# Four output stores per batch tile instead of five, through the same circular buffer

## The chip, the cores and the metric

One core of one Trainium2 chip. The metric is the device time of one execution in microseconds (us), median of several runs, lower is better. Each set of runs has the kernel before in its own rounds (medians 1341.10 to 1341.41 us), and every kernel is compared with that one unless the text says otherwise.

## The reference, cut to what matters

A pairwise bilinear interaction over 32 fields of 64 numbers, for a batch of 4096. Every pair (i, j) with i < j has its own 64 x 64 matrix.

```python
i_idx, j_idx = np.triu_indices(32, k=1)          # 496 pairs
vi, vj = inputs[:, i_idx, :], inputs[:, j_idx, :]
vdotw = jnp.einsum('bpd,pde->bpe', vi, W)
return (vdotw * vj).reshape(B, -1)               # 4096 x 31744 f32, 520 MB
```

The output is 520 MB and the input 42 MB. The work is in writing the result.

## The kernel before

The batch is cut into 32 tiles of 128 rows, one row for each SBUF partition. Fields are taken two at a time ("pair p" is fields 2p and 2p + 1, p = 0 to 15). TensorE multiplies into PSUM (the memory that takes its results), VectorE multiplies that by x and writes the product into a circular buffer (the ring), and the sync engine sends each finished stretch of the ring to HBM. One store carries the pairs of one group, so its row in each partition is the sum of their widths.

```python
STORES = [[0, 1], [2, 3], [4, 5], [6, 7, 8], [9, 10, 11, 12, 13, 14, 15]]
PREFETCH_AT = [5, 6]       # pairs at which the next tile is transposed
RING = 28160               # f32 words in each partition, 110 KB
...
for t in range(NT):
    ...                                            # x of tile t + 1 is loaded (ScalarE's queue)
    for s, group in enumerate(STORES):
        if at + store_w[s] > RING:
            at = 0                                 # the rest of the ring is skipped
        osb = ring[:, at : at + store_w[s]]
        at += store_w[s]
        for p in group:
            ...                                    # matmuls -> PSUM; VectorE: osb = PSUM * x
        nc.sync.dma_start(out=out[ts(t, P), o0 : o0 + store_w[s]], in_=osb)
```

A VectorE instruction that writes a stretch of the ring must wait until the older stores that read that stretch have landed. All pairs of a tile together are 31744 words, more than the ring holds.

Of the kernel before, what the change touches and what calls it, by code (L numbers as in the profile page):

```python
# [1 line left out]

# [6 lines left out]

F32 = mybir.dt.float32  # L10
ALU = mybir.AluOpType

P = 128
BANK = 512

STORES = [[0, 1], [2, 3], [4, 5], [6, 7, 8], [9, 10, 11, 12, 13, 14, 15]]
PREFETCH_AT = [5, 6]
RING = 28160


@with_exitstack
def pair_bilinear_kernel(
    ctx: ExitStack,
    tc: tile.TileContext,
    x: bass.AP,
    w: bass.AP,
    out: bass.AP,
    F: int,
    D: int,
):  # L30
















    nc = tc.nc
    B = x.shape[0]
    NT = B // P
    NPR = F // 2  # L50

    width = [(F - 1 - i) * D for i in range(F)]
    off = [sum(width[:i]) for i in range(F)]
    woff = [sum(width[0 : 2 * p : 2]) for p in range(NPR)]
    store_w = [sum(width[2 * p] + width[2 * p + 1] for p in g) for g in STORES]

    const = ctx.enter_context(tc.tile_pool(name="const", bufs=1))
    xpool = ctx.enter_context(tc.tile_pool(name="x", bufs=2))
    xtpool = ctx.enter_context(tc.tile_pool(name="xT", bufs=2))
    psum = ctx.enter_context(tc.tile_pool(name="ps", bufs=4, space=bass.MemoryType.PSUM))  # L60

    ident = const.tile([P, P], F32, tag="ident", name="ident")
    make_identity(nc, ident)

    def runs(tl, a, b, n):

        ap = tl[:, a : a + n]
        return bass.AP(ap.tensor, ap.offset, [list(ap.ap[0]), [b - a, 2], list(ap.ap[1])])

    def load_x(t):  # L70
        xt = xpool.tile([P, F * D], F32, tag="x", name=f"x_{t}")
        nc.scalar.dma_start(out=xt, in_=x[ts(t, P), :])
        return xt

    def transpose_x(xT, t, xt, g):

        n = 2 * BANK // P
        pt = psum.tile([P, 2 * BANK], F32, tag="ps", name=f"pt_{t}_{g}")
        for c in range(n):
            nc.tensor.transpose(pt[:, ts(c, P)], xt[:, ts(n * g + c, P)], ident)  # L80
        nc.scalar.copy(xT[:, ts(g, 2 * BANK)], pt)  # L81

    def new_xT(t):
        return xtpool.tile([P, NPR * P], F32, tag="xT", name=f"xT_{t}")

    ring = const.tile([P, RING], F32, tag="ring", name="ring")
    at = 0
    xs = {0: load_x(0)}

    w_sb = []  # L90
    for p in range(NPR):
        wp = const.tile([P, width[2 * p]], F32, tag=f"w{p}", name=f"w{p}")
        nc.sync.dma_start(out=wp, in_=w[:, woff[p] : woff[p] + width[2 * p]])
        w_sb.append(wp)

    xTs = {0: new_xT(0)}
    for g in range(2):
        transpose_x(xTs[0], 0, xs[0], g)

    for t in range(NT):  # L100
        xt, xT = xs.pop(t), xTs.pop(t)
        if t + 1 < NT:
            xs[t + 1] = load_x(t + 1)
        for s, group in enumerate(STORES):
            if at + store_w[s] > RING:
                at = 0
            osb = ring[:, at : at + store_w[s]]
            at += store_w[s]
            o0 = off[2 * group[0]]
            for p in group:  # L110
                if t + 1 < NT and p in PREFETCH_AT:
                    if t + 1 not in xTs:
                        xTs[t + 1] = new_xT(t + 1)
                    transpose_x(xTs[t + 1], t + 1, xs[t + 1], PREFETCH_AT.index(p))
                for c0 in range(0, width[2 * p], BANK):
                    pm = psum.tile([P, 2, BANK], F32, tag="ps", name=f"pm_{t}_{p}_{c0}")
                    n = [max(0, min(BANK, width[2 * p + h] - c0)) for h in range(2)]
                    for h in range(2):
                        if n[h]:
                            nc.tensor.matmul(  # L120
                                pm[:, h, : n[h]],
                                xT[h * D : (h + 1) * D, ts(p, P)],
                                w_sb[p][h * D : (h + 1) * D, c0 : c0 + n[h]],
                                start=True,
                                stop=True,
                            )
                    o = [off[2 * p + h] - o0 + c0 for h in range(2)]
                    xj = [(2 * p + h + 1) * D + c0 for h in range(2)]
                    if n[0] == n[1]:
                        nc.vector.tensor_tensor(  # L130
                            runs(osb, o[0], o[1], n[0]),
                            pm[:, :, : n[0]],
                            runs(xt, xj[0], xj[1], n[0]),
                            ALU.mult,
                        )
                    else:
                        for h in range(2):
                            if n[h]:
                                nc.vector.tensor_tensor(  # L139
                                    osb[:, o[h] : o[h] + n[h]],  # L140
                                    pm[:, h, : n[h]],
                                    xt[:, xj[h] : xj[h] + n[h]],
                                    ALU.mult,
                                )
            nc.sync.dma_start(out=out[ts(t, P), o0 : o0 + store_w[s]], in_=osb)


# [33 lines left out]
```

## Time and profile before

| | before |
|---|---|
| time, median of 3 | 1341.25 us (1340.96 to 1341.39) |
| DMA, mean over the span | 420 GB/s |
| VectorE, TensorE busy | 88%, 86% |
| VectorE's wait for ring space | 93.0 us in 53 waits |
| store, issue to landing (median) | 22.4 us |

How to read it: each row of a store is one packet in the DMA records, 128 rows over 16 DMA engines are 8 rows an engine, and a store has landed when all 16 engines are done. The lines are shown in the prediction.

### The profile page before, as it was taken

Reading aid. Unit: us, or ns where it says so; the run is one execution under the profiler, and the core shown is the slowest. Engines: PE = TensorE matmul, PEld = TensorE weight load, DVE = VectorE, ACT = ScalarE, POOL = GpSimd, SP = SyncE. Lnnn points to the kernel's source line nnn. Section 1 sums busy time; section 2 is a strip of 40 time slices with the busy share of each in tenths; the row PEclk is TensorE's granted clock in tenths of the full one; section 3 lists DMA queues with packets and bytes.
Section 4 is the critical chain, followed back from the end, with each engine's and each line's share of the span. In section 5 each row is a group of like instructions: output and inputs, shape, how many; then the busy total and the mean of one; then the engine's idle time right before and its main releaser. Section 6 shows DMA issues by size and latency. Waiting matters only on the chain.

```text
span 1339.7 us, 13755 instructions
## 1 busy us (share of the span) xinstructions
PE 1151.0 (86%) x5376; PEld 548.7 (41%) x5376; DVE 1177.4 (88%) x1664; ACT 66.1 (5%) x65; POOL 0.7 (0%) x6
## 2 busy tenths in 40 slices
PE   7998889888898888988888978889798897888992
PEld 3444344443343443443433534444344443444441
DVE  6999889888899988989888989899898997898993
ACT  1000000000000000000000000000000000000000
POOL 0000000000000000000000000000000000000000
PEclk9999889999999999989999899899898998998996
DMA  9999999999999999999999999999999999999996
GB/s 392 426 431 434 429 431 429 427 427 434 426 434 430 422 422 430 422 424 429 415 426 424 426 426 404 415 420 431 428 420 408 431 427 431 416 424 420 422 429 264
DMA packets 30017, 562.93 MB, mean 420 GB/s; under 512 B 3456, under 2 KB 3840, under 8 KB 5376
## 3 DMA queue, kind: packets, MB, share of 16 engines
q1 hardware_dynamic: 25344, 528.49, 92.6%
q10 hardware_dynamic: 4608, 33.56, 6.0%
q8 instruction: 42, 0.69, 0.2%
q14 instruction: 23, 0.19, 0.0%
HBM read 41.94 MB, written 520.09 MB: 420 GB/s over the span
## 4 chain that ended last, share of the span: by engine, by line
DMA 54%; DVE 23%; PE 11%; issue 9%; DVEq 0%
DMA out_dram<-ring 54%; DVE ring L130 15%; PE pm L120 9%; DVE ring L139 9%; PE pt L80 2%; DMA x<-in_x_dram 1%; DVEq L130 0%; DVEq L177 0%
## 5 line engine op out<-in xcount | busy, mean ns | idle before, releaser
L120 PE MATMUL pm<-w,xT 64*128 64x512 f32 (+7 forms) x4864 | 1083.2, 559 | 158.3 <-DVE ring L130 140.1
L130 DVE TENSOR_TENSOR ring<-pm,x 128x1024 f32<-128x1024 f32 x768 | 904.0, 1217 | 138.4 <-DMA out_dram<-ring 93.0
L120 PEld LDWEIGHTS pm<-w,xT 64*128 64x128 f32 x4864 | 487.7, 194 | 720.1 <-DVE ring L130 451.3
L139 DVE TENSOR_TENSOR ring<-pm,x 128x448 f32<-128x448 f32 (+6 forms) x896 | 330.2, 415 | 3.6 <-PE pm L120 2.9
L81 ACT COPY xT<-pt 128x1024 f32<-128x1024 f32 x64 | 64.8, 1012 | 1194.6 <-PE pt L80 1194.6
L80 PE MATMUL pt<-ident,x 128*128 128x128 f32 x512 | 76.5, 297 | 8.5 <-DMA x<-in_x_dram 8.5
L80 PEld LDWEIGHTS pt<-ident,x 128*128 128x128 f32 x512 | 61.0, 152 | 48.9 <-issue 35.3
L81 ACT ACT_TABLE_LOAD x1 | 1.3, 1283 | 1.7 <-PEq L173 1.7
masks.py:199 POOL TENSOR_SCALAR_AFFINE_SELECT ident<-ident 128x128 f32<-128x128 f32 x1 | 0.3, 292 | 0.1
masks.py:197 POOL MEMSET ident<- 128x128 f32 x1 | 0.2, 204 | 0.3 <-POOLq L173 0.3
L173 POOL MEMSET const-bfloat16-1.0<- 128x1 bf16 x1 | 0.1, 101 | 0.0
L173 POOL MEMSET const-uint8-127<- 128x1 uint8 x1 | 0.1, 101 | 0.0
L173 POOL MEMSET const-float32-0.0<- 128x1 f32 x1 | 0.1, 98 | 0.2 <-issue 0.2
L173 POOL MEMSET const-float32-1.0<- 128x1 f32 x1 | 0.1, 98 | 0.0
## 6 DMA issues: line engine op xcount, KB each, us to landing
out_dram<-ring SPq DMA_DIRECT2D x32, 3776.0 KB, 22.8
out_dram<-ring SPq DMA_DIRECT2D x32, 3264.0 KB, 21.8
out_dram<-ring SPq DMA_DIRECT2D x32, 3168.0 KB, 22.4
out_dram<-ring SPq DMA_DIRECT2D x32, 2912.0 KB, 22.3
out_dram<-ring SPq DMA_DIRECT2D x32, 2752.0 KB, 22.1
x<-in_x_dram ACTq DMA_DIRECT2D x32, 1024.0 KB, 14.2
w<-in_w_dram SPq DMA_DIRECT2D x1, 992.0 KB, 7.4
w<-in_w_dram SPq DMA_DIRECT2D x1, 928.0 KB, 11.7
```

What stands on the lines that cost most here:

```text
L80: nc.tensor.transpose(pt[:, ts(c, P)], xt[:, ts(n * g + c, P)], ident)
L81: nc.scalar.copy(xT[:, ts(g, 2 * BANK)], pt)
L120: nc.tensor.matmul(pm[:, h, : n[h]], xT[h * D : (h + 1) * D, ts(p, P)], w_sb[p][h * D : (h + 1) * D, c0 : c0 + n[h]], start=True, stop=True,)
L130: nc.vector.tensor_tensor(runs(osb, o[0], o[1], n[0]), pm[:, :, : n[0]], runs(xt, xj[0], xj[1], n[0]), ALU.mult,)
L139: nc.vector.tensor_tensor(osb[:, o[h] : o[h] + n[h]], pm[:, h, : n[h]], xt[:, xj[h] : xj[h] + n[h]], ALU.mult,)
L173: nc = bacc.Bacc("TRN2", target_bir_lowering=False, num_devices=1)
```

## The change

Its intent: one transfer fewer in each tile, and longer rows (26 to 39 KB instead of 22 to 30 KB), so less overhead on the queue that sets the time. Pair 6 moves to the third store, and the last two stores become one.

```diff
-STORES = [[0, 1], [2, 3], [4, 5], [6, 7, 8], [9, 10, 11, 12, 13, 14, 15]]
+STORES = [[0, 1], [2, 3], [4, 5, 6], [7, 8, 9, 10, 11, 12, 13, 14, 15]]
```

## The prediction

> **What bounds the kernel now.** I read the page's engine sums first, then the slices, the DMA queues, the chain, and last the waits and the closing 40 us.
>
> ```profile
> PE 1151.0 (86%) x5376; PEld 548.7 (41%) x5376; DVE 1177.4 (88%) x1664; ACT 66.1 (5%) x65; POOL 0.7 (0%) x6
> ...
> PEclk9999889999999999989999899899898998998996
> DMA  9999999999999999999999999999999999999996
> ...
> q1 hardware_dynamic: 25344, 528.49, 92.6%
> q10 hardware_dynamic: 4608, 33.56, 6.0%
> q8 instruction: 42, 0.69, 0.2%
> ...
> DMA out_dram<-ring 54%; DVE ring L130 15%; PE pm L120 9%; DVE ring L139 9%; PE pt L80 2%; DMA x<-in_x_dram 1%; DVEq L130 0%; DVEq L177 0%
> ```
>
> The DMA row is at 9 or above in every slice but the last, and the queue shares add to about 99%. VectorE and TensorE are at 88% and 86%: behind, but not far. The chain goes through stores for 54% and through VectorE and TensorE for the rest, so I need to know whether those stretches are a second limit or only a filled-up ring seen from the other side.
>
> ```profile
> PEld pm L120 <- DVE ring L130: 451.3, 535, 4.2
> ...
> DVE ring L130 <- DMA out_dram<-ring: 93.0, 53, 3.3
> DVE ring L130 <- PE pm L120: 45.4, 52, 13.2
> ```
>
> VectorE waits 93 us for ring space, that is for a store to land, and 45 us for TensorE, of which 13 are the start. Tile 0 has no ring waits and takes VectorE 36.9 us; a tile in the middle takes about 41. So compute is faster than the stores, and the ring throttles it.
>
> ```profile
> DMA  9999989998972999999999989893000000100000
> GB/s 422 392 422 412 422 351 585 404 404 356 422 334 92 406 406 406 406 402 529 576 426 395 395 371 400 375 584 165 25 25 25 23 23 23 47 23 23 23 0 0
> ...
> out_dram<-ring SPq DMA_DIRECT2D x1, 2752.0 KB, 22.4
> ```
>
> This is the window of the last 40 us, one slice a microsecond. After 1328 us the DMA moves about 25 GB/s: one engine of 16 is alone for ten more microseconds. From the trace's packet records, the last rows of each store on that engine end about 1.5 us after the others in tile 0, 8 us after at 550 us, and stay near 10 from then on. One engine falls behind, and a store has landed only when that one is done; the others then run dry waiting for the ring. So the bound is **the one late DMA engine**, and it never runs dry: each of its rows follows the last one directly to 1338.4.
>
> Its account: the packets of the big stores are whole rows, with median durations 818, 865, 940, 968 and 1119 ns for 22016, 23296, 25344, 26112 and 30208 B. A line through the shortest and longest has 301 ns for 8192 B (27.2 B/ns) and leaves 818 - 22016 x 0.03674 = 9 ns per row. Each engine carries 8 rows of each store: 8 x 4710 = 37.68 us a tile, plus 8 rows of x at 309 ns (2.47) and six 9 ns completion packets: 40.2. Times 32: 1286.6. The weights are 20.6 (8 x the sum of 16 medians). That is 1307 for any engine. The 42 instruction fetches of 16 KB are 42 x 16384 / 27.2 = 25.3 us if all sit on one engine, which would make the late one. Sum 1332.5; the first packet comes at 2 us, the last ends at 1338.4, so some 4 us are start-up gaps. The account closes.
>
> **What the Trainium skill says.** "DMA: Bandwidth & Descriptors", section "Specifications", gives 435 GB/s for 16 engines; 16 x 27.2 B/ns is 435, so the trace agrees and the engines already run at their ceiling inside a row. The same page, section "Why a DMA increments its semaphore by 16 and not by 1": only the full 16 means that all data landed; the trace agrees, with 2816 4-byte packets on the store queue, 16 for each of 176 transfers, and landings set by the latest. Its section "Anatomy of one DMA" gives a fixed cost of about 2.0 us per DMA, mostly the write receipt, fitted on another path. In this trace what lies outside the data is 0.83 us from issue to first packet on idle engines and 0.6 us from completion packet to VectorE's start; with transfers queued behind one another none of it is engine time. Its section "Queues, rings and completion order" has each engine taking turns between queues packet by packet; the x loads agree: first packet about 4 us after issue, then 8 rows in 10 us, about (0.31 + 0.94) x 8.
>
> **The change part by part.** Pair 6 moves from the fourth store to the third, and the last two stores become one. Compute instructions, their order and all bytes stay. Rows are 30208, 26112, 31488 and 39168 B.
> - Removed: 32 stores. One fewer row packet for each partition and tile, 8 per engine: 8 x 9 ns = 72 ns; one completion packet, 9 ns. 81 ns x 32 = **2.6 us of the late engine's time**. New rows at the same line: 31488 B 1166 ns, 39168 B 1448 ns; 8 x (1119 + 968 + 1166 + 1448) = 37.61 us a tile against 37.68.
> - Issue on the sync engine: 332 ns x 32 fewer, off the path (0).
> - Ring: 7552, 6528, 7872 and 9792 words in 28160. The allocation repeats every three tiles; it skips up to 6208 words at the wrap and often keeps only three stores in flight instead of four. This can add time, but only if the late engine runs dry.
>
> The tightest place by hand: tiles 0, 3, 6..., last store at words 0 to 9792, over the same tile's first store (0 to 7552). VectorE must wait for that landing at pair 7. The late engine then holds the second and third stores: 8 x (968 + 1166) = 17.1 us. VectorE needs 0.6 to start, 11.6 for pairs 7 to 15 (tile 0: 36.8 - 25.3), 0.83 to the first packet: 13.0. **4 us are left.** Its later ops, from word 7552 on (pair 11), need the second store, 7.7 us after the first; VectorE gets there at 8.6, so no second wait. In tiles 1, 4, 7... the last store is at 7872 to 17664 and about 5 us are left; elsewhere 6 or more. The same count for before, first store of tile 4 over the second of tile 3: 8 x (818 + 940 + 865) = 21.0, less 0.6, 8.5 and 0.83, is 11. The lead of the other engines stops at about 10 there, which is what this margin should cap it at; so the counting seems sound.
> - Ramp: the third store is issued at about 38.5 instead of 35.4, while the second lands at 46.7; the fourth at 50.6, with the third in flight to about 56. No gap.
> - End: the last store takes 11.6 us instead of 6.9 on an engine, but the late one still has most of the third store before it when it is issued, as it has now (issued at 1319.5, its turn comes at 1331.5). 0.
>
> Sum: 1341.25 - 2.6 = **1338.6 us**, 0.2% less.
>
> **The rivals.**
> (a) The fixed cost goes away: 32 x 2.0 (the skill's figure, an estimate) = 64 us, 1277 us. For: bigger transfers are the usual advice. Against: stores are queued, issue to landing 22 us for 7 to 9 us of data, and the engines show no gap between stores in the first 450 us. I give it one in a hundred.
> (b) The coarse ring starves the late engine. For: margin falls from about 10 to 4 us, and VectorE has PE waits of 1 to 2.5 us after many ring waits. If the tight place is short by 2 us in two tiles of three, 21 x 2 = 42 us, 1381; short by 1 us in one of three, 11 us, 1350. Against: after a ring wait TensorE has four PSUM tiles ready, pairs 7 to 15 hold no transposes, and 4 us is more than the largest such wait.
> (c) x arrives late. Rows of 1.17 to 1.45 us between its own: 4.7 + 8 x (0.31 + 1.17 to 1.45) = 16.5 to 18.8 us instead of 14, while TensorE reaches the transposes 16.8 us after a tile's start when nothing stops it (least slack before: 1.8 us). It waits up to 2 us in some tiles; the tile then takes 39 of 41 us, so 0 on the end, unless it adds to (b).
> (d) Long rows go slower or are cut in two. Cut: 9 ns a row, back to 0. The line is straight up to 30208 B, so slower is unlikely.
>
> **Range and chances.** The saving is small and sure if the margin holds; the tail is on the slow side, from (b) with (c). Range 1335.5 to 1347. Faster by over 2%: 0.01. Slower by over 2% needs 27 us, about 0.85 us in each tile: 0.05. Within 2%: 0.94.
>
> **What would show it.** Right: 20736 packets on the store queue; row medians near 1166 and 1448 ns; a late engine with no gap; the lone engine's stretch at the end shorter, about 4 to 6 us instead of 10, since the others' lead is now capped at the margin, and more dips of the DMA row in the middle; ring waits of VectorE again about 80 to 120 us in total, fewer but longer; x landing at 16 to 18 us. Wrong: the lone stretch gone and gaps on all 16 engines together after a ring wait (b); waits of the transposes for x above 2 us a tile (c); row medians off the line (d).

## More of the kernel before

Where this document speaks of single DMA engines, the packets of the trace, which carry no engine number, were sorted into 16 chains: each engine takes 8 rows of every store in order, and the next row starts within a few ns of the end of the last one. About 240 of the 256 x rows of an engine were placed, so such sums are good to about a microsecond.

## The result, and the profile after

| | before | after |
|---|---|---|
| time, median of 6 | 1341.36 us | 1339.97 us (1339.69 to 1340.18) |
| ratio | | 0.999 (0.9977 to 1.0003) |
| VectorE's wait for ring space | 93.0 us, 53 waits, longest 3.3 | 104.3 us, 40 waits, longest 5.0 |
| TensorE's wait for x | 8.5 us, once | 42.9 us, 25 waits |
| x load, issue to landing (median) | 14.2 us | 18.1 us |

The ratio is the mean time of one kernel's runs over that of the other's of the same rounds, so it is not quite the ratio of the medians. Its interval contains 1, but no run of one kernel falls into the other's range. The gain is 1.4 us, 0.1%.

The queues of the changed kernel on its page (packets, MB, share of 16 engines' time):

```profile
span 1338.1 us, 13641 instructions
...
DMA  9999999999999999999999999999999999999998
...
q1 hardware_dynamic: 20736, 528.49, 92.5%
q10 hardware_dynamic: 4608, 33.56, 6.0%
q8 instruction: 42, 0.69, 0.2%
```

The store queue lost 25344 - 20736 = 4608 packets, which is 32 tiles x (128 rows + 16 completion packets), and moved the same bytes. In the packet records the new rows took 1166 and 1448 ns (medians of 31488 and 39168 B), the figures that the prediction had drawn from the line.

Its waits, from the view of who waited for whom (total us, times, longest):

```profile
DVE ring L130 <- DMA out_dram<-ring: 104.3, 40, 5.0
...
PE pt L80 <- DMA x<-in_x_dram: 42.9, 25, 8.5
DVE ring L130 <- PE pm L120: 36.8, 37, 14.2
```

Ring waits became fewer and longer. The wait of the transposes (line 80) for x is new: before there was only the 8.5 us of the start. The other 24 waits are 0.5 to 2.6 us long, five of them over 2. The chain of work that ended last shows it too: x has 12% of it, where it had 1% before.

```profile
DMA out_dram<-ring 34%; DVE ring L130 16%; PE pm L120 15%; DVE ring L139 12%; DMA x<-in_x_dram 12%; PE pt L80 3%; DVEq L130 0%; DVEq L177 0%; DVEq L139 0%
```

The last 40 us of the changed kernel, one slice a microsecond (busy tenths and GB/s):

```profile
DMA  9976999999999999999949999399499399220000
GB/s 483 453 332 272 453 483 404 422 422 408 444 392 418 418 482 493 467 472 504 441 189 472 472 557 572 157 580 509 196 548 548 157 548 588 118 118 0 39 0 0
```

Before, one engine went on alone for ten slices at 25 GB/s. Now the others stay busy until a few microseconds before the end. Sorted by engine, the late one ended at 1336.8 us and the others around 1333.0, where before it was 1338.4 and 1327.9. The late engine itself is done 1.6 us earlier. A small part of that is not the rows: the changed kernel has 114 instructions fewer (13641 for 13755) and one 8 KB instruction fetch fewer (28 for 29, those before the span counted), which at 27.2 B/ns is an estimated 0.3 us. The others ran dry more often in the middle, as a window of 800 to 840 us shows, first of the kernel before, then of the changed one:

```profile
DMA  8969998999999989989962999999999999599999
```

```profile
DMA  1949939999999999999999992999991919194995
```

The low slices are not lost time: they are the 15 other engines waiting, while the late one works.

### The profile page after: what moved, and what is told of

Read it like the earlier page. It is cut to its first block, busy times and chain, and to the rows that moved or that the text cites. A ratio compares the mean times of both kernels' runs of the same rounds, so it can differ in the third digit from the quotient of the medians.

```text
span 1338.1 us, 13641 instructions
## 1 busy us (share of the span) xinstructions
PE 1142.2 (85%) x5376; PEld 530.4 (40%) x5376; DVE 1175.7 (88%) x1664; ACT 66.1 (5%) x65; POOL 0.7 (0%) x6
## 3 DMA queue, kind: packets, MB, share of 16 engines
q1 hardware_dynamic: 20736, 528.49, 92.5%
q10 hardware_dynamic: 4608, 33.56, 6.0%
## 4 chain that ended last, share of the span: by engine, by line
DMA 45%; DVE 28%; PE 18%; issue 7%; DVEq 0%
DMA out_dram<-ring 34%; DVE ring L130 16%; PE pm L120 15%; DVE ring L139 12%; DMA x<-in_x_dram 12%; PE pt L80 3%; DVEq L130 0%; DVEq L177 0%; DVEq L139 0%
## 5 line engine op out<-in xcount | busy, mean ns | idle before, releaser
L130 DVE TENSOR_TENSOR ring<-pm,x 128x1024 f32<-128x1024 f32 x768 | 904.7, 1219 | 144.2 <-DMA out_dram<-ring 104.3
L120 PEld LDWEIGHTS pm<-w,xT 64*128 64x128 f32 x4864 | 473.2, 190 | 707.9 <-DVE ring L130 445.1
L80 PE MATMUL pt<-ident,x 128*128 128x128 f32 x512 | 72.2, 286 | 43.0 <-DMA x<-in_x_dram 42.9
L80 PEld LDWEIGHTS pt<-ident,x 128*128 128x128 f32 x512 | 57.2, 145 | 79.9 <-issue 79.9
## 6 DMA issues: line engine op xcount, KB each, us to landing
x<-in_x_dram ACTq DMA_DIRECT2D x32, 1024.0 KB, 18.1
```

The costliest lines, as they stand in the source:

```text
L80: nc.tensor.transpose(pt[:, ts(c, P)], xt[:, ts(n * g + c, P)], ident)
L120: nc.tensor.matmul(pm[:, h, : n[h]], xT[h * D : (h + 1) * D, ts(p, P)], w_sb[p][h * D : (h + 1) * D, c0 : c0 + n[h]], start=True, stop=True,)
L130: nc.vector.tensor_tensor(runs(osb, o[0], o[1], n[0]), pm[:, :, : n[0]], runs(xt, xj[0], xj[1], n[0]), ALU.mult,)
```

## The experiments

Theory A: one DMA engine is later than the rest and sets the time; a store costs that engine only its row starts and completion packets; the ring may be coarser as long as that engine never runs dry. Rivals: the time is all bytes over 16 engines; a store has a large fixed cost; the ring is close to its limit anyway; the longer rows or the later x cost something.

### What a store costs

Eight stores a tile, with rows of 10 to 25 KB (5 rounds; the diff here and in the next two runs is against the changed kernel, the time against the kernel before with its five stores):

```diff
-STORES = [[0, 1], [2, 3], [4, 5], [6, 7, 8], [9, 10, 11, 12, 13, 14, 15]]
+STORES = [[0], [1], [2], [3], [4], [5], [6, 7, 8], [9, 10, 11, 12, 13, 14, 15]]
```

> The kernel before with 8 stores a tile, rows of 10 to 30 KB (pairs 0 to 5 alone). The run with 14 stores cost 106 ns for each store and tile, more than either theory, but it also ran into a wait of the issuing engine for earlier stores (355 times) and into late x loads, which this one should not. Theory A, 46 ns: 3 x 46 x 32 = +4.4 us, 1345.8. Theory B, 81 ns: +7.8 us, 1349. If the 106 ns of the 14-store run hold for all sizes: +10.2 us, 1351.5.

Measured 1346.33 us against 1341.16, +5.2 us: 5.2 / (3 x 32) = 54 ns for a store and tile. The 95% interval of the ratio is 3.4 to 7.1 us, which holds theory A's 4.4 (46 ns) and not 7.8 (81 ns). Why 46: in the trace a row of 39168 B is recorded with 1448 ns, but the next row on that engine starts 1445 ns after it; the same 3 or 4 ns overlap stands behind every size. So a row start costs about 5 ns and a completion packet 6, not 9 each. One more 8 KB instruction fetch (30 for 29) may be 0.3 of the 5.2 us, by the same estimate.

Fourteen stores a tile, one for each pair and one for the last three (3 rounds):

```diff
+STORES = [[0], [1], [2], [3], [4], [5], [6], [7], [8], [9], [10], [11], [12], [13, 14, 15]]
```

> The kernel before with 14 stores a tile instead of 5 (one per pair, the last three pairs together). The change took away one store a tile and gained 1.4 us where 2.6 had been predicted. Theory A: a store costs the late DMA engine only its 8 row starts and one completion packet, and the distance from one row's start to the next row's is about 4 ns less than the recorded duration, so 8 x 5 + 6 = 46 ns a store and tile; 9 more stores in 32 tiles give +13 us, about 1354.5. Theory B (the prediction's sizes, 9 ns a row and 9 a completion): 81 ns, +23 us, about 1365. Theory C (a fixed cost of about 2 us for every store is on the path): +580 us. The ring is no limit here under any theory, since smaller stores only widen its margin.

Measured 1371.94 us, +30.5 us or 106 ns for a store and tile: more than theories A and B, and far from C. The run brought in other things. The sync queue's own waits and the waits of TensorE:

```profile
SPq L145 <- DMA out_dram<-ring: 931.1, 355, 6.5
```

```profile
PE pt L80 <- DMA x<-in_x_dram: 87.5, 25, 8.5
```

The issuing engine waited 355 times for an earlier store to land, which the kernel before, the changed one and the one with eight stores never did, and x came late although rows were short. A row of x took 354 ns in the mean instead of 311. What lengthened it was not settled; the run only refutes a fixed cost of microseconds.

Half of the change, pair 6 moved but still five stores (5 rounds):

```diff
+STORES = [[0, 1], [2, 3], [4, 5, 6], [7, 8], [9, 10, 11, 12, 13, 14, 15]]
```

> Half of the change: pair 6 goes to the third store (now 31 KB rows), but the last two stores stay apart, so five stores as before. Theory A (only the number of stores counts): no change from before, within 0.3 us, 1341.3. Rival (the new boundaries or the longer x loads behind long rows matter): other than that.

Measured 1341.48 against 1341.16: no change. Moving pair 6 alone gains nothing; the gain comes with the store fewer.

### Why one engine is late

Instructions added to ScalarE (3 rounds):

```diff
+EXTRA = 9
...
+                for _ in range(EXTRA):             # for each pair
+                    nc.scalar.copy(junk, one)      # one element
```

> The kernel before with 4608 one-element copies added on ScalarE, an engine that is 5% busy; no other engine gets work and no data moves. Theory A (one DMA engine also fetches the instructions, and this is why it is late and sets the time): the program's instruction bytes grow by about a third (50 to 64 B an instruction, 0.23 to 0.3 MB), 14 to 18 more 16 KB fetches of 0.6 us on that one engine: +8 to +11 us, with the same lone engine at the end. Rival (the time is the sum of all bytes over all 16 engines, and the lone engine at the end is an accident of the last stores): 0.3 MB at 420 GB/s is 0.7 us, so no change within 1 us.

Measured 1669.61 us. The run is spoilt: ScalarE also moves the transposes out of PSUM, in order behind the 4608 copies of 0.19 us, and everything waited for it.

```profile
ACT 55%; DMA 17%; issue 10%; DVE 10%; PE 6%; ACTq 0%; DVEq 0%
ACT junk L116 53%; DMA out_dram<-ring 16%; DVE ring L136 6%; PE pm L126 5%; DVE ring L145 4%; ACT xT L85 2%; PE pt L84 1%; DMA x<-in_x_dram 0%; ACTq L76 0%; DVEq L136 0%; DVEq L183 0%
```

The chain of that run goes through the copies (line 116) for 53% of the span. It says nothing on the question, except that queue 14 had 36 more 8 KB packets: 4608 x 64 B.

The same number of instructions on GpSimd, which nobody waits for (3 rounds):

```diff
+EXTRA = 9
...
+                for _ in range(EXTRA):             # for each pair
+                    nc.gpsimd.memset(junk, 1.0)    # one element
```

> The kernel before with 4608 one-element memsets on GpSimd, which has no other work after the start and which nobody waits for. (The run with ScalarE copies was spoilt: ScalarE also moves the transposes out of PSUM, and TensorE and VectorE waited for it. It did show 36 more 8 KB instruction fetches on queue 14, which is 4608 x 64 B.) Theory A (one DMA engine also serves the instruction fetches and this makes it late): 36 more fetches of 8 KB at 27.2 B/ns, 0.30 us each, on that engine: +10.8 us, 1352. Rival (the time is all bytes over 16 engines): +0.7 us, so 1342.

Measured 1355.95 us against 1341.16, +14.8 us, where the rival allows 0.7. The queues of its page, then its last 40 us:

```profile
q8 instruction: 42, 0.69, 0.2%
q14 instruction: 59, 0.48, 0.1%
```

```profile
DMA  9999999979992999999998999898001000000100
GB/s 418 418 418 547 456 433 387 409 327 488 484 418 113 399 402 428 402 398 423 398 398 368 390 645 417 371 394 371 25 25 50 23 23 23 23 23 23 46 0 0
```

Queue 14 went from 23 packets to 59, 0.29 MB, and the kernel ends again with one engine alone for ten slices. Sorted by engine, over the first five tiles after the first (when the others do not yet wait for it) the late one needed 210.9 us instead of 206.2, and the median engine about 201 in both. VectorE was not slowed by GpSimd: busy 1178.2 us against 1177.4. The lengthened rows of this engine, read next, also end with the added instructions: on the store of pairs 0 and 1, the eight to ten rows of a tile that are longer than the rest are so by 61 to 80 ns (median) in tiles 1 to 15, against 32 to 43 before; the last memset ran at 677 us, and from tile 17 to tile 30 both kernels have 30 to 44. So instruction bytes fall on one engine, and that engine sets the time.

How they fall on it is different from what I had thought. The 16 KB and 8 KB packets are in the records, but the late engine shows no pause of that length for most of them. Instead nearly every store row on it is longer than the same row on the others, by 14, 23, 33, 42 ns and so on, steps of about 9.4 ns, the time of 256 B at 27.2 B/ns. The lengthenings add up to 32.05 us before; the recorded fetches after the start, 42 x 16 KB + 23 x 8 KB = 0.88 MB, are 32.2 us at 27.2 B/ns. In the run with GpSimd instructions the lengthenings are 46.4 us, 14.35 more, so within the sorting error they carry the +14.7 us of the late engine. That is 4 us more than the added bytes at that rate explain (10.8); this remainder is open.

x loads on fewer engines (3 rounds):

```diff
-        nc.scalar.dma_start(out=xt, in_=x[ts(t, P), :])
+        nc.scalar.dma_start(out=xt[0:120, :], in_=x[t * P : t * P + 120, :])
+        nc.scalar.dma_start(out=xt[120:128, :], in_=x[t * P + 120 : t * P + 128, :])
```

> The kernel before, with each x load cut into 120 partitions and 8 partitions. By the engine-count rule the 120 rows go over 15 engines, 8 rows each, and the last 8 rows over 8 engines, one row each. If the late engine is the one left out it loses 8 x 0.31 x 32 = 79 us of x and the bound becomes the next engine's load, about 1307 + 10 + start-up: 1318 to 1325. If the late engine is among the 8 that get one more row: +10 us, about 1351. If it is among the others: no change. Rival (bytes over 16 engines): no change or a slight loss in every case.

Measured 1362.59 us, +21.2. From the last row of the first tile to that of the last tile, the late engine needed 1282.0 us instead of 1268.9: 13.1 us, 0.4 us a tile, near the one more x row of 0.31 us. The x queue had 736 completion packets, 23 a tile instead of 16, which fits 15 engines for the one piece and 8 for the other. So it is one of the first eight, if transfers on fewer engines use the lowest-numbered ones, as the Trainium skill says ("DMA: Bandwidth & Descriptors", section "Why a DMA increments its semaphore by 16 and not by 1"); the trace has no engine numbers to confirm it. The other 9 us are at the start, which I had left out: the second piece of x waited among the weight loads, VectorE began at 18.8 us instead of 13.2, and the late engine ended the first tile 9 us later. On that reading the late engine cannot be spared by this cut, since a transfer on fewer engines keeps the first ones.

### How close the ring is

Both kernels with the ring cut from 28160 to 23552 words (3 rounds each):

```diff
-RING = 28160
+RING = 23552
```

> The changed kernel (four stores) with a ring of 23552 words instead of 28160. Theory A (the four-store kernel is fast only because about 4 us of margin are left at the last store of a tile): with this ring the last store of a tile must wait for the store just before the one in front of it, the margin becomes negative every tile, and all DMA engines run dry: a hand count of the queue gives some 5 to 7 us a tile, 1500 to 1560 us in all. Rival (the ring is not close to a limit, DMA time is bytes over rate): no change, 1340.

> The kernel before (five stores) with the ring of 23552 words that took the four-store kernel to 1645 us. Theory A (what matters is the margin left by the grain of the stores, and five smaller stores still have some 6 to 9 us of it in this ring): 1341, unchanged. Rival (the smaller ring itself is too small for the latency of a store, whatever the grain): clearly slower, 1400 or more.

Measured: four stores 1644.51 us, five stores 1341.96. The ring waits, of four stores and then of five:

```profile
DVE ring L130 <- DMA out_dram<-ring: 369.9, 79, 9.7
DVE ring L130 <- PE pm L120: 49.7, 83, 14.0
```

```profile
DVE ring L130 <- DMA out_dram<-ring: 110.8, 50, 4.2
```

And a window of 800 to 840 us of the four-store kernel in the small ring:

```profile
DMA  0999990999000000090909193990919399999999
GB/s 26 504 504 504 504 504 0 504 504 504 0 0 0 0 0 0 0 627 0 758 0 758 57 700 131 627 758 0 758 49 678 131 492 461 483 483 483 483 483 483
```

Here the zeros are all 16 engines dry for seven slices in a row, not 15 of them waiting for one. In this ring, from the second tile on, the last store of a tile lies partly on the store just before it, must wait for it to land, and then nothing is left in the queue. Five stores in the same ring lose 0.8 us at most. So it is the grain of the stores, not the size of the ring alone, that makes the cliff. My hand count gave 1500 to 1560, some 100 us too few. It had taken the pace of VectorE from tile 0, without restarts after long waits; whether that is the reason was not tested.

Four stores, ring of 24576 words (3 rounds):

```diff
-RING = 28160
+RING = 24576
```

> The changed kernel with a ring of 24576 words. Between 28160 (1340 us) and 23552 (1645 us) the hand count of the queue has the allocation repeat every two tiles: at the second tile's first store 1.6 us of margin are left and at its second store -0.3, or about -1.3 if a ring wait costs VectorE and TensorE another 1 us to get going. Theory A: 0.3 to 1.3 us lost in every second tile, so 1345 to 1361, between the four-store kernel and the cliff. Rival (anything under 28160 is over the cliff): over 1500. Rival (ring words only matter at the cliff): 1340.

Measured 1407.06 us, outside what every theory gave, on the side of A: past the edge, not yet down the cliff. The window of 218 to 258 us, where a tile starts on a store that has yet to land:

```profile
DMA  3999990009299590929959099998399999999999
GB/s 157 504 504 504 504 504 0 16 0 627 123 635 523 235 758 0 758 123 635 523 235 758 0 615 483 483 453 362 151 483 483 483 418 418 418 408 418 418 418 418
```

The engines are dry in several short stretches, and every second tile takes about 46 us instead of 40.5 (from landing to landing of its first store). I had counted the tight store alone. Once the queue is empty, the next store in this order needs VectorE longer than the one before it occupies the DMA (pairs 4 to 6: 9.4 us of compute behind a store of 7.7; pairs 7 to 15: 11.6 behind 9.3), so the engines run dry at the following stores too. These numbers fit; no run tests them alone.

Three stores in the full ring, the next step in the direction of the change (3 rounds):

```diff
+STORES = [[0, 1, 2], [3, 4, 5, 6], [7, 8, 9, 10, 11, 12, 13, 14, 15]]
```

> The next step in the direction of the change: three stores a tile (pairs 0 to 2, 3 to 6, 7 to 15) in the full ring of 28160 words. Theory A: one store fewer saves another 1.5 us of the late engine, but the ring holds only two of these stores beside the one being written, the margin is about -4 us in each tile, and all engines run dry: 1400 to 1440, perhaps more, as the hand count was 100 us too low for the small ring. Rival (fewer, bigger stores go on paying): 1338.5.

Measured 1491.25 us, 11% slower than the kernel before. VectorE's waits for the ring:

```profile
DVE ring L130 <- DMA out_dram<-ring: 241.8, 82, 6.7
```

The direction is refuted beyond four stores; the size of the loss was again more than counted by hand.

### What the late x costs

The transposes of the next tile three pairs later, with four stores (3 rounds) and with five (5 rounds):

```diff
-PREFETCH_AT = [5, 6]
+PREFETCH_AT = [8, 9]
```

> The changed kernel (four stores) with the transposes of the next tile at pairs 8 and 9 instead of 5 and 6, some 8 us later in the tile. In the changed kernel TensorE waits 43 us in total for x, against 8.5 before. Theory A (these waits lie inside the time that the ring gives back, since the late DMA engine never runs dry): the x wait falls to the 8.5 us of the start and the ring wait grows by about as much; the time stays 1340 within 0.5 us. Rival (the x waits are what ate half of the predicted 2.6 us): 1 to 2 us faster, 1338.5.

> The kernel before (five stores) with the transposes of the next tile at pairs 8 and 9, as in the run with four stores that came to 1338.8. There it gained 1.2 us. If the gain comes from TensorE's waits for x, which five stores don't have (8.5 us, all at the start), nothing changes here: 1341.3. If it comes from something that has nothing to do with the number of stores, such as where the other instructions and their fetches fall, it gains about as much here: 1340.1.

Measured: four stores 1338.76 us (1338.62 to 1338.86), five stores 1341.25. The waits with four stores and later transposes:

```profile
DVE ring L130 <- DMA out_dram<-ring: 101.8, 42, 4.0
...
PE pt L80 <- DMA x<-in_x_dram: 8.8, 1, 8.8
```

The x waits are gone, the ring waits did not grow, and the kernel is 1.2 us faster than with four stores and early transposes (1339.97, in other rounds, whose kernels before agree within 0.03 us). x has 1% of its chain again. With five stores, which had no x waits, the same edit changed nothing. So my theory, that these waits lie wholly inside the time that the ring gives back, falls for the four-store kernel: taking them away gained 1.2 us. The 12% of the chain that x has in the changed kernel point to the waits; through which path they made the late engine later is open. The late engine shows no idle stretch in either run, and the differences in its sums (0.3 us at the start, about 1.6 in lengthened rows, some 0.3 to 0.5 the other way) are of the size of the sorting error. This kernel, four stores with the transposes at pairs 8 and 9, is the fastest: 2.6 us ahead of the kernel before in the same rounds (1341.33), ratio 0.9981 (0.9966 to 0.9996).

## Why the prediction was right or wrong, point by point

- **The bound.** Right. One DMA engine sets the time; it has no gap in the changed kernel either, and adding instruction bytes to it moved the end by 14.8 us while adding 0.05% to the bytes.
- **Its account.** The sum closed for a partly wrong reason. It had 25.3 us for the 16 KB fetches and "some 4 us" of start-up gaps. The 8 KB fetches of queue 14 fall on this engine too; with both, 32 us of lengthened rows stand in the trace, and much of the 4 us was theirs.
- **The saving, 81 ns a store and tile, 2.6 us.** The direction was right, the sum mis-sized: 1.4 us, or 1.4 / 32 = 43 ns. Two steps can have failed, and the runs do not say how the missing 1.2 us divide between them. One is "9 ns per row": it was the constant of a line through recorded durations, and consecutive rows overlap by 3 to 4 ns. Start to start gives about 5 ns a row and 6 a completion packet, 46 ns in all; eight stores measured 54. The other is the 0 for late x (below): later transposes gave back 1.2 us, the whole of what was missing. With later transposes five stores to four gave 2.5 us, 78 ns (2.7 us and 85 ns, if each is taken against the kernel before of its own rounds), which is the predicted 81. So the size of a store is shown to be between about 45 and 85 ns, and not closer; that the kernel with later transposes comes to the predicted 1338.6 within 0.2 us does not tell the two apart.
- **The ring.** Right. The count of 4 us of margin was seen as the lead of the other engines, which stops at about 3.5 to 5 us in the changed kernel as it stopped at about 10 before. Rival (b) did not happen at 28160 words, but it is close: at 24576 it costs 5%.
- **x (rival c).** Half right. Landing at 18.1 us came as counted, and the waits came, 1.4 us in the mean; but five of 24 were above the 2 us that the prediction had named as a sign of being wrong, the longest 2.6. "So 0 on the end" failed: later transposes gained 1.2 us with four stores and nothing with five.
- **Fixed cost (a) and row speed (d).** Right: neither shows. Row durations lay on the line to the nanosecond.
- **End and ramp.** Right: the last store was issued at 1320.0 us against 1319.5 before, and the lone stretch shrank to about 4 us.

## What to carry to other kernels

In this kernel, where transfers queue behind one another, the fixed cost of one was already hidden, and merging them gave back only about 45 to 85 ns for each store and tile on the busiest engine. Merging is paid for with the grain of the buffer: before making stores bigger, count how much is left in the queue when the store that must be waited for has landed, against the compute time of the store being filled; keep that positive for every place in the ring. And when one DMA engine finishes alone, look for what only it carries before looking at average bandwidth.

## What the Trainium skill lacked or had wrong

- "DMA: Bandwidth & Descriptors", section "Anatomy of one DMA", gives about 2.0 us fixed for a DMA, fitted on another path. In a full queue a store cost 43 to 85 ns of time here (five to four and five to eight stores); that section has no figure for this case.
- The same page, "Latency and other measured facts", has engines 7 and 15 usually slower, with a best guess tied to descriptor rings of GpSimd's path. No data went by that path here, yet one engine was 1.0 us a tile slower (41.2 against 40.2 in the first tiles); the trace has no engine numbers, so it may or may not be engine 7.
- That instruction fetches load one of the 16 data engines is on no page; it belongs to "Runtime: NRT & Kernel Launch", section "Instruction fetch mechanics". Here 4608 more GpSimd instructions made the kernel 14.8 us slower.
- "Perfetto Trace Analysis", section "DMA Optimizations", has batching of small transfers, with examples of 2 to 8 KB, as the main remedy when DMA-bound. It does not say where that ends: with rows of 22 KB and more, five to four stores gave 0.1% here, and four to three cost 11%, because of the buffer.
